# Evening out GpSimd's work over the four steps of an attention group

## The chip, the core and the metric

The kernel runs on one core of a Trainium2 chip. The metric is the device time of one execution in microseconds (us). A core has five engines that work through queues of their own, each in the order in which its instructions were issued: TensorE (PE in the profile; its weight loads are PEld), VectorE (DVE), ScalarE (ACT), GpSimd (POOL) and SyncE (SP, which here only starts transfers). They wait for each other through semaphores. An instruction that waits holds up everything behind it on its engine. Transfers (DMAs) are started from the queues of SP and POOL and then run by themselves.

## What is computed

Eight sequences of 512 tokens with 256 features go through four blocks, each added to its input: attention A, a feed-forward, attention B and the same feed-forward again. All of it is in float32. The change is in attention A only:

```python
# attention A, per token: 16 heads of 64 channels
Q = (x @ Wq + bq).reshape(b, s, H, C) * inv_sqrt_c
K = (x @ Wk + bk).reshape(b, s, H, C)
V = (x @ Wv + bv).reshape(b, s, H, C)
scores = jnp.einsum('bshq,bshk->bshqk', Q, K)
mask = jnp.triu(jnp.ones((C, C), dtype=bool), 1)
scores = jnp.where(mask, jnp.asarray(-jnp.inf, scores.dtype), scores)
w = jax.nn.softmax(scores, axis=-1)
attn = jnp.einsum('bshqk,bshk->bshq', w, V)
...
x = x + _L0_attn_a_ref(_layernorm(x), ...)
x = x + _L0_ffn_ref(_layernorm(x), ...)
x = x + _L0_attn_b_ref(_layernorm(x), ...)
x = x + _L0_ffn_ref(_layernorm(x), ...)
```

This attention is unusual: it works between the 64 channels of one head of one token. Each token and head has its own 64x64 triangle of scores, an outer product of a row of Q and a row of K. There is nothing to multiply as a matrix, so the scores, the exponentials, the products with V and the row sums are element by element work for DVE, GpSimd and ACT.

## The kernel before

Tokens lie on the 128 partitions, so a batch (one sequence) has four tiles of 128 tokens, `i`. The 16 heads are taken in four groups of four heads, `g`, so 256 columns a group. A pair (g, i) is called a group in this text; there are 16 in a batch and 128 in all. The triangle under the diagonal of each head is cut into squares: one of 32x32, two of 16x16, four of 8x8 and so on. A group is worked in four units `u`, one for each step of the schedule (line 553):

- unit 0: the squares of 32 of two heads, in a tile `w` (three buffers, shared with unit 2)
- unit 1: the squares of 16 of all four heads, in a tile `w16` (one buffer)
- unit 2: the squares of 32 of the other two heads, in a tile `w`
- unit 3: the squares of 8, 4, 2 and 1, in a tile `ws` (one buffer)

A tile holds the scores (later their exponentials) and beside them their products with V. Every unit goes through stages, and `step(n)` (line 638) issues one stage of several units, so that units follow each other as in a pipeline. "Step 0" to "step 3" below means a step by the unit whose scores it issues. A step has three parts, with a `yield` after each; between parts the schedule slips in instructions of the other blocks. The stages of a unit are:

- `scores` (line 765): the products of q and k. Units 0 and 2 run on GpSimd, which reads a copy of q and k in SBUF, in two pieces; units 1 and 3 run on DVE, which reads q from PSUM. The group's diagonal (`acc`, L771) goes with unit 0, on DVE.
- `exps` (line 789), one step later: exponentials on ACT.
- `weigh` (line 800), two steps later: products with V on DVE (L808; L805 for the diagonal).
- `halve` (line 810), in the same step: for units 0, 1 and 2 a DMA started by GpSimd adds one half of the tile onto the other (L814, 1 MB).
- `fold` (line 816): for units 0 and 2, GpSimd adds the remaining halves once more (L819). It waits for that DMA.
- `gather` (line 838): DVE sums along the rows (L845). Unit 1's gather waits for unit 1's DMA, those of units 0 and 2 for the folds.
- `add_rows` (line 848): GpSimd adds the sums to the group's numerators and denominators in `acc` (L852). `small_squares` (line 828) is the same for the squares of 2 and 1 on GpSimd.
- `invert` and `divide` (lines 854 and 858): a reciprocal on DVE (L856), once per group, and a product on GpSimd (L860).

The order of PE, DVE, ACT and GpSimd is the order in which this code is called (`manual_schedule`, line 1341); the order on SP is left to the scheduler. For one group, from the calls of `step`, the order in the kernel before is:

| step | DVE | GpSimd |
|---|---|---|
| 0 | weigh 2, diagonal, reciprocal | scores 0 (first piece), start DMA of 2, scores 0 (second piece), divide, fold 0 |
| 1 | weigh 3, gather 1, scores 1 (two pieces), gather 0 | add of the 16s, small squares and their adds, fold 2 |
| 2 | weigh 0, gather 2, gather 3 | scores 2 (first piece), start DMA of 0, scores 2 (second piece), add of unit 0's 32s |
| 3 | weigh 1, scores 3 | start DMA of 1, adds of unit 2's 32s, of the 8s and of the 4s |

The numbers are units; units 2 and 3 in steps 0 and 1 belong to the group before, as do all folds, gathers and adds of sums.

The main loop (lines 1347 to 1354) takes attention A one batch ahead of the other blocks. During the first batch attention A runs alone. From then on, the feed-forward, attention B and second feed-forward of one batch are slipped in between the parts of the next batch's steps (`after_a`, 309.5 units of estimated work for each 64 steps). The last batch's other blocks run alone at the end.

At the beginning there is work that happens once. `fit_qkv` (line 339) subtracts a row from the weights of a head group (on DVE for the first, on GpSimd for the three others) and stores them. `later_weights` (line 411) is a generator, `prep` in the main loop, that prepares other weights: three rounds on a bias row (L421 to L428), products on w3 (L451), on wbqk and wbvp (L456) on GpSimd, and at its end `bound_scores` (line 359), which loads the q, k and v weights again, squares them on ACT (L373 and L374) and sums them on PE (L382), to see whether the scores are bounded. `measure` (line 726) takes the mean and variance of a batch's tokens. Blocks of 8 KB per partition for such data come from a pool of seven (`hp`).

Of the kernel before, what the change touches and what calls it, by code (L numbers as in the profile page):

```python
# [9 lines left out]
F32 = mybir.dt.float32  # L10
# [3 lines left out]
ALU = mybir.AluOpType  # L14
AX = mybir.AxisListType

P = 128
# [9 lines left out]
GW = GH * C  # L27
NG = HID // GW
# [256 lines left out]
def fast_path(ctx: ExitStack, tc: tile.TileContext, k, t, flag):  # L285

    nc = tc.nc
# [8 lines left out]
    ap_ = ctx.enter_context(tc.tile_pool(name="ap", bufs=2))  # L296
# [270 lines left out]
    def pieces(w, n, off, nsq, cols):  # L567

        def of_rows(v):
            return v[:, cols].rearrange("p (x t) -> p x t", t=2 * n)[:, :, n:]

        def of_cols(v):
            return v[:, cols].rearrange("p (x t) -> p x t", t=2 * n)[:, :, :n]

        if n < 16:
            e, ev = (  # L580
                w[:, a * SMALL + off : a * SMALL + off + nsq * n * n].rearrange("p (x i j) -> p x i j", i=n, j=n)
                for a in range(2)
            )
            yield e, ev, lambda v: of_rows(v).unsqueeze(3), lambda v: of_cols(v).unsqueeze(2)
            return
        both = w.rearrange("p (b a x i j) -> p a b x i j", a=2, x=nsq, i=n, j=JB)
        if n == 32:
            for x in range(nsq):
                yield (
                    both[:, 0, :, x],  # L590
                    both[:, 1, :, x],
                    lambda v, x=x: of_rows(v)[:, x].unsqueeze(1).unsqueeze(3),
                    lambda v, x=x: of_cols(v)[:, x].rearrange("p (b j) -> p b j", j=JB).unsqueeze(2),
                )
        else:
            for k in range(n // JB):
                yield (
                    both[:, 0, k],
                    both[:, 1, k],
                    lambda v: of_rows(v).unsqueeze(3),  # L600
                    lambda v, k=k: of_cols(v)[:, :, k * JB : (k + 1) * JB].unsqueeze(2),
                )

    class AttentionA:
# [33 lines left out]
        def step(self, n):  # L638

            weighed = self.at(n - 2)  # L640
            if weighed[0] is not None:
                self.weigh(*weighed)
            unit = self.at(n)
            on_pool = unit[3] in (0, 2)
            if on_pool:
                half = self.scores(*unit)
                next(half)
            if weighed[0] is not None:
                self.halve(*weighed)
            if on_pool:  # L650
                next(half, None)
            b, i, g, u = self.at(n + 40)
            if u == 0 and g == 0 and i == 0 and b > 0:
                self.x[b] = load_x(b)
            b, i, g, u = self.at(n + 10)
            if u == 0 and g == 0 and i == 0:
                self.measure(b)
            b, i, g, u = self.at(n + 8)
            if u == 0 and g == 0:
                self.live["xn"] = normed(self.x[b][:, i, :], *self.rn[b, i], "a")  # L660
            b, i, g, u = self.at(n - 5)
            if u == NU - 1:
                self.invert(b, i, g)
            b, i, g, u = self.at(n - 4)
            if u == 1:
                self.gather(b, i, g, u)
            b, i, g, u = self.at(n + 7)
            if u == 0 and g == 0:
                nc.scalar.copy(self.live[b, i], self.live.pop("ps_ln"))
            if self.at(n - 1)[0] is not None:  # L670
                self.exps(*self.at(n - 1))
            yield
            if unit[0] is not None and not on_pool:
                for _ in self.scores(*unit):
                    pass
            for args in self.sums:
                self.add_rows(*args)
            self.sums = []
            b, i, g, u = self.at(n - 5)
            if u == NU - 1:  # L680
                self.divide(b, i, g)
            b, i, g, u = self.at(n - 2)
            if u == NU - 1:
                self.small_squares(b, i, g)

            b, i, g, u = self.at(n - 4)
            if u == 0:
                self.fold(b, i, g, u)
            b, i, g, u = self.at(n - 3)
            if u == 2:  # L690
                self.fold(b, i, g, u)
            b, i, g, u = self.at(n - 9)
            if u == NU - 1:
                self.new_x(b, i, g)
            b, i, g, u = self.at(n + 2)
            if u == 0:
                self.keep_qk(b, i, g)
            b, i, g, u = self.at(n - 7)
            if u == NU - 1:
                self.turn_group(b, i, g)  # L700
            b, i, g, u = self.at(n - 8)
            if u == NU - 1:
                self.project_out(b, i, g)
            b, i, g, u = self.at(n + 3)
            if u == 0:
                self.project(b, i, g)
            yield
            b, i, g, u = self.at(n - 4)
            if u == 2:
                self.gather(b, i, g, u)  # L710
            b, i, g, u = self.at(n - 5)
            if u == 0:
                self.gather(b, i, g, u)
            b, i, g, u = self.at(n - 3)
            if u == NU - 1:
                self.gather(b, i, g, u)
            b, i, g, u = self.at(n - 7)
            if u == NU - 1:
                nc.scalar.copy(self.live["att"], self.live.pop("pta"))
            b, i, g, u = self.at(n + 8)  # L720
            if u == 0 and g == 0:
                self.live[b, i] = lnp.tile([P, DC, P], F32, tag="xnt_a", name=f"xnta_{b}_{i}", bufs=NT)
                self.live["ps_ln"] = turned_over(self.live.pop("xn"), half_bank().rearrange("p (c s) -> p c s", c=DC))
            yield
# [40 lines left out]
        def scores(self, b, i, g, n_u):  # L765

            qv, kt = self.live[b, i, g][:2]
            if n_u == 0:
                acc = ap_.tile([P, 2, GW], F32, tag="acc", name=f"acc_{b}_{i}_{g}", bufs=3)
                self.live[b, i, g].append(acc)  # L770
                nc.vector.tensor_tensor(acc[:, 0, :], qv[:, 0], kt[:, 0], ALU.mult)  # L771

            if n_u in (0, 2):
                w = wt.tile([P, 4096], F32, tag="w", name=f"w_{b}_{i}_{g}_{n_u}", bufs=3)
            elif n_u == 1:
                w = wt.tile([P, 4096], F32, tag="w16", name=f"w16_{b}_{i}_{g}")
            else:
                w = wt.tile([P, 2 * SMALL], F32, tag="ws", name=f"ws_{b}_{i}_{g}")
            self.live[b, i, g, n_u] = w
            eng, q = (nc.gpsimd, kt[:, 1]) if n_u in (0, 2) else (nc.vector, qv[:, 0])  # L780
            for n, off, nsq, cols in squares(units[n_u]):
                for e, ev, rows, columns in pieces(w, n, off, nsq, cols):
                    shape = list(e.shape)
                    eng.tensor_tensor(  # L784
                        e, rows(q).to_broadcast(shape), columns(kt[:, 0]).to_broadcast(shape), ALU.mult
                    )
                    yield
# [50 lines left out]
        def gather(self, b, i, g, n_u):  # L838


            w = self.live.pop((b, i, g, n_u))
            for n, off, nsq, cols in squares(units[n_u]):
                if n > 2:
                    red = ap_.tile([P, 2, nsq * n], F32, tag=f"red{nsq * n}", name=f"red_{b}_{i}_{g}_{n_u}_{n}", bufs=2 + (n < 32))
                    nc.vector.tensor_reduce(red, self.columns_of(w, n, off, nsq), AX.X, ALU.add)  # L845
                    self.sums.append((b, i, g, n, cols, red))

        def add_rows(self, b, i, g, n, cols, part):

# [491 lines left out]
    with tc.manual_schedule(engines={ET.PE, ET.DVE, ET.Activation, ET.Pool}):  # L1341
        a = AttentionA()
        prep = later_weights()
        fit_qkv(0)
        weights = None
        done, spent = after_a(), 0
        for n in range(-10, a.steps):
            for part, _ in enumerate(a.step(n)):
                if n >= 2:
                    next(prep, None)  # L1350
                while 3 * spent * each < total * (3 * (n - each - 11) + part + 1):
                    spent += next(done)
            if 0 <= n < NG - 1:
                fit_qkv(n + 1)
        for _ in done:
            pass
    judge()
# [86 lines left out]
```

## Time and profile before

| | us |
|---|---|
| median of 3 runs (lowest, highest) | 4008.09 (4007.45, 4010.71) |
| the profiled execution | 4009.55 |
| its span, first to last instruction | 4007.6 |

Some groups of instructions of that execution (a span on GpSimd overlaps with the next by up to 0.3 us, so the distance from start to start is shorter than its mean):

| line, engine, what | count | busy us | mean ns |
|---|---|---|---|
| L784 POOL, scores of units 0 and 2 | 512 | 1076.2 | 2102 |
| L784 DVE, scores of unit 1 | 256 | 301.3 | 1219 |
| L808 DVE, weigh units 0, 1, 2 | 768 | 899.8 | 1213 |
| L819 POOL, folds | 256 | 643.1 | 2512 |
| L814 POOL, start of the adding DMA | 384 | 337.1 | 878 |
| L845 DVE, gathers of units 0 and 2 | 256 | 309.7 | 1210 |
| L845 DVE, gather of unit 1 | 128 | 292.0 | 2281 |
| L852 POOL, adds of 128x256 sums (16s, 8s, 4s) | 384 | 291.6 | 759 |
| L852 POOL, adds of 128x128 sums (32s) | 256 | 179.4 | 701 |
| L856 DVE, reciprocal | 128 | 223.2 | 1744 |

The profile shows for each engine when it was busy, and for each instruction what ended the idle time before it. A row of the timeline has the start and the length in us, the engine, the line of the kernel, the operation, what is written and read, and in brackets the idle time before it with what ended it. Tile names are cut: `w` stands for the tiles of units 0, 1 and 2, `ws` for unit 3. "red" is the sum tile of a gather. Shapes tell the units apart: a gather of 128x1024 from `w` is unit 0 or 2, of 128x2048 from `w` is unit 1.

### The profile page before, as it was taken

What the parts mean: (1) busy time and instruction counts of PE and PEld (TensorE: products, weight loads), DVE (VectorE), ACT (ScalarE), POOL (GpSimd) and SP (SyncE); (2) the same over time, 40 slices, a digit from 0 to 9 for tenths busy, and PEclk for the clock granted to TensorE, in tenths of its full rate; (3) what the DMA queues carried; (4) which work ended last, traced back from release to release, by engine and by line L of the source; (5) the groups of instructions that cost most, each with busy time, mean ns of one, the idle gap of its engine ahead of it and who ended that gap; (6) DMA issues with size and microseconds to landing.
All of it is one profiled execution on the core that took longest, in us unless ns stands there. A gap on an engine that the chain in (4) does not pass through costs nothing.

```text
span 4007.6 us, 37678 instructions
## 1 busy us (share of the span) xinstructions
PE 2958.0 (74%) x12328; PEld 2012.2 (50%) x12328; DVE 3376.7 (84%) x3777; ACT 2337.2 (58%) x3145; POOL 3098.1 (77%) x3051
## 2 busy tenths in 40 slices
PE   1543478777876888768787788768787778768988
PEld 0311145355653656346553566346653556436847
DVE  4899988998889888998989988998889988897115
ACT  2433465666755766666755767567656667555342
POOL 6688888887888887887888888888888878886211
PEclk7555689888987989889897889879898899879999
DMA  8566777668776777668776688668877687767304
GB/s 240 114 141 145 146 182 182 147 161 199 199 162 126 195 188 196 150 147 210 174 192 139 168 198 214 147 131 198 195 181 151 154 199 205 155 133 210 126 29 167
DMA packets 118653, 671.07 MB, mean 167 GB/s; under 512 B 12704, under 2 KB 31915, under 8 KB 43824
## 3 DMA queue, kind: packets, MB, share of 16 engines
q0 software_dynamic: 78336, 570.46, 62.9%
q1 hardware_dynamic: 40112, 98.11, 6.8%
q8 instruction: 100, 1.64, 0.2%
q14 instruction: 105, 0.86, 0.1%
HBM read 255.90 MB, written 9.96 MB: 66 GB/s over the span
## 4 chain that ended last, share of the span: by engine, by line
DVE 38%; PE 16%; POOL 14%; DMA 12%; issue 8%; ACT 8%; POOLq 0%; DVEq 0%; ACTq 0%
DVE red L845 15%; DMA w<-w 12%; DVE w L808 10%; PE ph L1120 5%; ACT w L798 3%; POOL w L819 3%; DVE ws L808 3%; POOL w L784 3%; PE pqkb L1167 3%; DVE ws L784 3%; POOL acc L852 3%; DVE w L784 2%; POOL w L814 2%; DVE acc L856 2%; POOL h L1036 2%
## 5 line engine op out<-in xcount | busy, mean ns | idle before, releaser
L798 ACT ACTIVATE w<-w 128x2048 f32<-128x2048 f32 x384 | 734.2, 1913 | 653.8 <-POOL w L784 440.8
L1120 PE MATMUL ph<-h,hidden 128*128 128x512 f32 x4096 | 1047.9, 412 | 77.4 <-POOL h L1036 45.5
L784 POOL TENSOR_TENSOR w<-k 128x1024 f32<-128x1024 f32 x512 | 1076.2, 2102 | 9.6 <-ACT k L762 9.0
L1120 PEld LDWEIGHTS ph<-h,hidden 128*128 128x128 f32 x4096 | 795.3, 196 | 282.1 <-POOL h L1036 55.9
L808 DVE TENSOR_TENSOR w<-w,qv 128x1024 f32<-128x1024 f32 x768 | 899.8, 1213 | 22.4 <-ACT w L798 22.3
L845 DVE TENSOR_REDUCE red<-w 128x128 f32<-128x1024 f32 (+1 forms) x384 | 601.8, 1567 | 171.6 <-DMA w<-w 94.6
L819 POOL TENSOR_TENSOR w<-w 128x1024 f32<-128x1024 f32 x256 | 643.1, 2512 | 72.5 <-DMA w<-w 71.9
L814 POOL DMA_DIRECT2D w<-w x384 | 337.1, 878 | 339.7 <-issue 134.8
L852 POOL TENSOR_TENSOR acc<-acc,red 128x256 f32<-128x256 f32 (+1 forms) x640 | 471.0, 736 | 152.3 <-DVE red L845 124.5
L845 DVE TENSOR_REDUCE red<-ws 128x256 f32<-128x2048 f32 (+1 forms) x256 | 435.5, 1743 | 0.0
L746 PE MATMUL qv<-wqv,xnta 128*128 128x512 f32 x512 | 299.3, 715 | 89.9 <-DVE ws L808 82.4
L808 DVE TENSOR_TENSOR ws<-ws,qv 128x1024 f32<-128x1024 f32 (+3 forms) x512 | 294.7, 638 | 49.4 <-ACT ws L798 49.4
L1052 PE MATMUL pw<-xnt,gate 128*128 128x512 f32 (+2 forms) x1152 | 298.8, 419 | 24.9 <-ACT silu L1028 18.0
L784 DVE TENSOR_TENSOR w<-qv,k 128x1024 f32<-128x1024 f32 x256 | 301.3, 1219 | 3.6
L784 DVE TENSOR_TENSOR ws<-qv,k 128x1024 f32<-128x1024 f32 (+3 forms) x512 | 299.8, 648 | 0.0
L868 PE MATMUL bank<-ident,acc 128*128 128x128 f32 x256 | 64.3, 341 | 287.5 <-ACT k L761 287.1
L798 ACT ACTIVATE ws<-ws 128x1920 f32<-128x1920 f32 x128 | 231.5, 1809 | 75.3 <-DVE ws L784 74.7
L1052 PEld LDWEIGHTS pw<-xnt,gate 128*128 128x128 f32 x1152 | 227.6, 213 | 82.1 <-ACT silu L1028 22.3
L1229 ACT ACTIVATE eb<-psb 128x256 f32<-128x256 f32 (+3 forms) x512 | 182.2, 443 | 146.6 <-PE psb L1226 146.3
L1146 PE MATMUL pof<-w,h 128*128 128x256 f32 x1024 | 247.9, 396 | 19.4 <-ACT h L1085 19.4
L1085 ACT ACTIVATE h<-ph,s_sb 128x512 fp32r<-128x512 f32 (+1 forms) x256 | 171.1, 688 | 145.9 <-PE ph L1120 144.6
L856 DVE RECIPROCAL acc<-acc 128x256 f32<-128x256 f32 x128 | 223.2, 1744 | 12.3 <-POOL acc L852 12.3
(143 smaller groups left out, 4723.5 us busy)
## 6 DMA issues: line engine op xcount, KB each, us to landing
w<-w POOLq DMA_DIRECT2D x384, 1024.0 KB, 7.7
hidden<-in_h POOLq DMA_DIRECT2D x128, 1024.0 KB, 7.9
gate<-in_w12p POOLq DMA_DIRECT2D x32, 1024.0 KB, 9.0
w<-w_d SPq DMA_DIRECT2D x16, 1024.0 KB, 12.0
wqv<-wqv_d SPq DMA_DIRECT2D x31, 512.0 KB
wo<-in_wo SPq DMA_DIRECT2D x32, 256.0 KB, 7.4
wbqk<-wbqk_d SPq DMA_DIRECT2D x8, 1024.0 KB
w<-in_h SPq DMA_DIRECT2D x8, 1024.0 KB, 7.0
```

Of the source, the lines that this page charges most:

```text
L746: nc.tensor.matmul(qv.rearrange("p j f -> p (j f)"), xnt[:, c, :], wqv[:, c, :], start=(c == 0), stop=(c == DC - 1),)
L784: eng.tensor_tensor(e, rows(q).to_broadcast(shape), columns(kt[:, 0]).to_broadcast(shape), ALU.mult)
L798: nc.scalar.activation(e, e, AF.Exp, scale=C**-0.5)
L808: nc.vector.tensor_tensor(ev, e, columns(qv[:, 1]).to_broadcast(list(e.shape)), ALU.mult)
L814: nc.gpsimd.dma_start(w[:, :2048], w[:, 2048:], accum_op=ALU.add)
L819: nc.gpsimd.tensor_tensor(w[:, :1024], w[:, :1024], w[:, 1024:2048], ALU.add)
L845: nc.vector.tensor_reduce(red, self.columns_of(w, n, off, nsq), AX.X, ALU.add)
L852: nc.gpsimd.tensor_tensor(rows, rows, part.rearrange("p a (x i) -> p a x i", i=n), ALU.add)
L856: nc.vector.reciprocal(acc[:, 0, :], acc[:, 0, :])
L1052: nc.tensor.matmul(pj[:, toks], w[:, m % 4, j, c, :], xs[:, p, c, toks], start=(p == 0 and c == 0), stop=(p == 1 and c == DC - 1),)
L1120: nc.tensor.matmul(pss[j], w[:, j, c, :], h_in(p, c), start=(p == 0 and c == 0), stop=(p == 1 and c == MC - 1),)
L1146: nc.tensor.matmul(po, h(0, c)[:, i * P : (i + 1) * P], w3[:, c, :], start=(c == 0), stop=False)
```

## The change

It has four edits in attention A and one in the main loop. (1) The first of the two score pieces of unit 1 is computed by GpSimd instead of DVE. (2) The sums of units 0 and 2 are written into one tile and added to `acc` together, once, after unit 2's gather. (3) The fold of unit 0 is issued at the end of step 3 instead of in the middle of the following step 0, and its gather at the end of step 0 instead of step 1. (4) The first batch's `measure` is called before the first `fit_qkv`. (5) `prep` takes one step for each step of the kernel (after its third part, from step number 3) instead of one after each part from step number 2, and the last three calls of `fit_qkv` come after step numbers 4, 14 and 24 instead of 0, 1 and 2.

With this, the table of a group reads (moved or new in capitals): step 0, GpSimd without the fold, DVE with GATHER 0 at its end; step 1, GpSimd begins with SCORES 1 (first piece), then the add of the 16s, small squares and fold 2 as before, DVE has one piece of scores 1 and no gather 0; step 2, GpSimd without an add; step 3, GpSimd has one add for all 32s, those of the 8s and 4s, and FOLD 0 at its end.

```diff
--- before.py
+++ after.py
@@ -654,7 +654,8 @@
                 self.x[b] = load_x(b)
             b, i, g, u = self.at(n + 10)
             if u == 0 and g == 0 and i == 0:
-                self.measure(b)
+                if b > 0:
+                    self.measure(b)
             b, i, g, u = self.at(n + 8)
             if u == 0 and g == 0:
                 self.live["xn"] = normed(self.x[b][:, i, :], *self.rn[b, i], "a")
@@ -683,9 +684,6 @@
             if u == NU - 1:
                 self.small_squares(b, i, g)
 
-            b, i, g, u = self.at(n - 4)
-            if u == 0:
-                self.fold(b, i, g, u)
             b, i, g, u = self.at(n - 3)
             if u == 2:
                 self.fold(b, i, g, u)
@@ -706,14 +704,13 @@
                 self.project(b, i, g)
             yield
             b, i, g, u = self.at(n - 4)
-            if u == 2:
-                self.gather(b, i, g, u)
-            b, i, g, u = self.at(n - 5)
-            if u == 0:
+            if u in (0, 2):
                 self.gather(b, i, g, u)
             b, i, g, u = self.at(n - 3)
             if u == NU - 1:
                 self.gather(b, i, g, u)
+            if u == 0:
+                self.fold(b, i, g, u)
             b, i, g, u = self.at(n - 7)
             if u == NU - 1:
                 nc.scalar.copy(self.live["att"], self.live.pop("pta"))
@@ -777,9 +774,11 @@
             else:
                 w = wt.tile([P, 2 * SMALL], F32, tag="ws", name=f"ws_{b}_{i}_{g}")
             self.live[b, i, g, n_u] = w
-            eng, q = (nc.gpsimd, kt[:, 1]) if n_u in (0, 2) else (nc.vector, qv[:, 0])
             for n, off, nsq, cols in squares(units[n_u]):
-                for e, ev, rows, columns in pieces(w, n, off, nsq, cols):
+                for p, (e, ev, rows, columns) in enumerate(pieces(w, n, off, nsq, cols)):
+
+                    on_pool = n == 32 or n == 16 and p == 0
+                    eng, q = (nc.gpsimd, kt[:, 1]) if on_pool else (nc.vector, qv[:, 0])
                     shape = list(e.shape)
                     eng.tensor_tensor(
                         e, rows(q).to_broadcast(shape), columns(kt[:, 0]).to_broadcast(shape), ALU.mult
@@ -841,9 +840,15 @@
             w = self.live.pop((b, i, g, n_u))
             for n, off, nsq, cols in squares(units[n_u]):
                 if n > 2:
-                    red = ap_.tile([P, 2, nsq * n], F32, tag=f"red{nsq * n}", name=f"red_{b}_{i}_{g}_{n_u}_{n}", bufs=2 + (n < 32))
-                    nc.vector.tensor_reduce(red, self.columns_of(w, n, off, nsq), AX.X, ALU.add)
-                    self.sums.append((b, i, g, n, cols, red))
+                    if n_u != 2:
+                        self.live["red", n] = ap_.tile(
+                            [P, 2, GW // 2], F32, tag=f"red{n // 32}", name=f"red{n}_{b}_{i}_{g}", bufs=1 if n == 32 else 3
+                        )
+                    red = self.live["red", n]
+                    part = red[:, :, cols.start // 2 : cols.stop // 2]
+                    nc.vector.tensor_reduce(part, self.columns_of(w, n, off, nsq), AX.X, ALU.add)
+                    if n_u != 0:
+                        self.sums.append((b, i, g, n, slice(0, GW), red))
 
         def add_rows(self, b, i, g, n, cols, part):
 
@@ -1341,17 +1346,18 @@
     with tc.manual_schedule(engines={ET.PE, ET.DVE, ET.Activation, ET.Pool}):
         a = AttentionA()
         prep = later_weights()
+        a.measure(0)
         fit_qkv(0)
         weights = None
         done, spent = after_a(), 0
         for n in range(-10, a.steps):
             for part, _ in enumerate(a.step(n)):
-                if n >= 2:
+                if n >= 3 and part == 2:
                     next(prep, None)
                 while 3 * spent * each < total * (3 * (n - each - 11) + part + 1):
                     spent += next(done)
-            if 0 <= n < NG - 1:
-                fit_qkv(n + 1)
+            if n in (4, 14, 24):
+                fit_qkv(n // 10 + 1)
         for _ in done:
             pass
     judge()
```

## The prediction

> **What bounds the kernel now.** I read the page's busy shares and 40 slices first, then busy time by windows, then the timelines of VectorE (DVE) and GpSimd (POOL) through one group, and last the waits.
>
> ```profile
> PE 2958.0 (74%) x12328; PEld 2012.2 (50%) x12328; DVE 3376.7 (84%) x3777; ACT 2337.2 (58%) x3145; POOL 3098.1 (77%) x3051
> ...
> DVE  4899988998889888998989988998889988897115
> POOL 6688888887888887887888888888888878886211
> ```
>
> DVE is busiest, GpSimd close behind; both fall away only in the last four slices, where the last batch's feed-forward and attention B run alone (TensorE's part, untouched by the change).
>
> ```profile
> 300.00:400.00 100.00, 37.65 (x64) 17.93 (x64) 99.73 (x108) 39.00 (x38) 85.25 (x78) 0.50 0.71 147
> ...
> 1393.90:1424.20 30.30, 25.62 (x98) 20.28 (x99) 23.92 (x26) 21.55 (x23) 22.14 (x20) 0.86 0.82 207
> ```
>
> (Columns: window, its length, busy time of PE, PEld, DVE, ACT, POOL; granted clock, DMA share, GB/s.) Attention A alone keeps DVE 99.7% busy. A group under a feed-forward takes 30.3 us with no engine full. The group's one reciprocal (L856) marks the period: of 127 intervals, 27 are short (mean 23.7 us), 21 middling (25.7, mostly under attention B), 78 long (30.4, feed-forward), and the first is 55.2. Here are DVE and GpSimd in a short group, from step 1 to step 3:
>
> ```profile
> 1250.14 2.29 DVE L845 TENSOR_REDUCE red<-w 128x256 f32<-128x2048 f32 x1 [0.60 <-DMA w<-w]
> 1252.46 2.36 DVE L784 TENSOR_TENSOR w<-qv,k 128x1024 f32<-128x1024 f32 x2
> 1254.73 1.21 DVE L845 TENSOR_REDUCE red<-w 128x128 f32<-128x1024 f32 x1
> 1255.86 0.41 DVE L805 TENSOR_TENSOR acc<-acc,qv 128x256 f32<-128x256 f32 x1
> 1256.19 2.34 DVE L808 TENSOR_TENSOR w<-w,qv 128x1024 f32<-128x1024 f32 x2
> 1258.45 1.21 DVE L845 TENSOR_REDUCE red<-w 128x128 f32<-128x1024 f32 x1
> 1259.58 3.40 DVE L845 TENSOR_REDUCE red<-ws 128x256 f32<-128x2048 f32 x2
> 1262.90 2.34 DVE L808 TENSOR_TENSOR w<-w,qv 128x1024 f32<-128x1024 f32 x2
> ```
> ```profile
> 1252.57 0.73 POOL L852 TENSOR_TENSOR acc<-acc,red 128x256 f32<-128x256 f32 x1 [0.53 <-DVE red L845]
> 1253.26 0.61 POOL L835 TENSOR_TENSOR ws<-ws 128x256 f32<-128x256 f32 x1
> 1253.95 1.66 POOL L852 TENSOR_TENSOR acc<-acc,ws 128x256 f32<-128x256 f32 x2
> 1255.57 2.37 POOL L819 TENSOR_TENSOR w<-w 128x1024 f32<-128x1024 f32 x1
> 1257.90 1.95 POOL L784 TENSOR_TENSOR w<-k 128x1024 f32<-128x1024 f32 x1
> ```
>
> Read them together. At 1252.43 DVE ends the reduce of the squares of 16 ("gather 16"). GpSimd, waiting for it, runs adds, small squares and the second fold until 1257.94. DVE has its own work until 1258.45, when it needs that fold for the reduce at 1258.45 ("gather 2"). The handshake closes with 0.5 us to spare; that margin is what the change touches.
>
> **What the Trainium skill says.** "GPSIMD Engine Reference", section 3.1, has a tensor_tensor of 2048 fp32 at 4497 ns on GpSimd and 2293 ns on VectorE, 1.96 times; here 1024 elements (L784) take 2102 and 1219 ns, 1.72 times: agreed roughly. "Perfetto Trace Analysis", GPSIMD Engine Instruction, advises start-to-start spacing over reported spans; the trace agrees (L784's mean is 2102 ns, the spacing 1.90 to 1.97), so I use spacings. "SBUF — State Buffer", Who interferes with whom, says a DVE tensor_tensor with both inputs in SBUF contends with GpSimd's reads; DVE's half keeps q in PSUM, and the 2.36 us pair above is undisturbed, so I add nothing for it.
>
> **The change, part by part** (spacings from these timelines).
>
> 1. Half of unit 1's scores to GpSimd. DVE loses 1.14 us a group (half of 2.27), GpSimd gains 1.95. The w16 tile has one buffer, so GpSimd's half must wait for gather 16 to have read the previous group's. In the compiled order it stands before the add of the 16s, the small squares and the fold of unit 2, so all of these queue behind that wait.
> 2. One add of 128x256 (0.70) replaces two of 128x128 (0.41 and about 0.7): GpSimd minus 0.4. The single buffer of the shared 32-square sums is free a fold before it is rewritten: nothing.
> 3. Fold of unit 0 (2.35) moves from step 0 to the end of step 3; its DVE reduce ("gather 0", 1.12) from step 1 to step 0. The fold now follows its DMA's issue by about 8 us instead of 13.5 (POOL timeline: issue at 1211.89; adds end at 1220.5; old fold at 1225.68). That DMA lands in 7.1 us (median, 200 to 500 us) and mostly 7.7 to 8.1 in the long groups I looked at. About even; a late landing stalls scores of unit 0 and the next DMA issue behind it.
>
> Sums for a short group: DVE 23.72 - 1.14 = 22.58; GpSimd about 21.1 + 1.95 - 0.4 = 22.6. By busy time alone this is a gain of up to 1.1 us. But follow the handshake. After gather 16, GpSimd needs 0.14 (wait) + 1.95 (its half) + 5.37 (1252.57 to 1257.94, as now) = 7.45 us until the fold ends. DVE's work between gather 16 and gather 2 shrinks from 5.98 to 1.14 + 0.33 + 2.26 = 3.73, since half the scores and gather 0 left that stretch. DVE stalls 3.7 us. Nothing on DVE can overtake, and GpSimd's half cannot start sooner. The closed chain is 7.45 + 18.85 (gather 2 round to the end of the next gather 16: 17.73 now, plus gather 0's 1.12) = 26.3 against 23.72: plus 2.6 us.
>
> Short groups: 27 x 2.6 = 70 us. Middling: ACT or DMA waits on DVE hide some, I take 1.8, 21 x 1.8 = 38 us.
>
> Long groups. DVE now waits for DMA and folds here:
>
> ```profile
> POOL acc L852 <- DVE red L845: 124.5, 57, 23.4
> ...
> DVE red L845 <- DMA w<-w: 94.6, 39, 7.2
> ...
> DVE red L845 <- POOL w L819: 76.9, 30, 5.6
> ```
>
> Three kinds occur between 1300 and 1600 us. Where feed-forward work fills the stretch from gather 16 to gather 2 (13.9 us in one group, 10.6 in another), the longer GpSimd chain is covered, and GpSimd, freed of a fold in step 0, may arrive earlier: 0, or minus 1 to 2. Where that stretch is tight (7.1 us, three groups), plus 0.4 and gather 0's 1.1. Where unit 2's DMA lands late (12.7 to 16.7 us), the fold of unit 0 before its issue delays it by about 2. I bound the mean by minus 1.2 (all of the first kind) and plus 2.5 (all of the third), and take plus 1.0: 78 x 1.0 = 78 us.
>
> 4. The beginning. Now the loads and squares for the bound of the scores come so early that ACT stands in front of them:
>
> ```profile
> 107.15 1.06 ACT L374 ACTIVATE sk<-sk 128x1024 f32<-128x1024 f32 x1 [21.88 <-DMA sk<-in_wqkv]
> ```
>
> DVE then waits 24.7 us for ACT, and the first interval is 55.2 instead of 23.7: 31 us to win. One generator step per kernel step instead of three puts squares at step 19, loads a step ahead. The first moments go ahead of the q/v subtraction: some 3 us more. Against it: the three GpSimd fits (3.6 each) and w3/wbqk products (10) now lie in groups whose GpSimd chain is tight; and on SP's queue the load of w3 stands behind the next wk load, which waits for TensorE's projection, so GpSimd's first w3 product can wait a whole load (7 to 12 us for such loads on the page). I bound the gain by 0 and 35 and take 20.
>
> Sum: 70 + 38 + 78 - 20 = 166 us. The profiled run took 4009.55 us (span 4007.6), the median 4008.09: 4175 either way.
>
> **Rivals.**
> A, not slower: the lighter step 0 decides. If GpSimd is what is late at step 1 in nearly all long groups, moving 2.35 us of fold out and 1.95 in, with DVE's stretch 2.3 shorter, gains 1.2 net: 70 + 38 - 94 - 20 = -6, 4002 us. It decides from a gain of 1.1 us in the mean long group. For it: GpSimd waited for gather 16 in only 57 of 128 groups. Against: GpSimd merely in time already counts among the other 71, as in short groups, where the chain closes. A larger gain needs the short groups' chain not to close too.
> B, slower still: two folds each wait for their DMA in turn. Fold 0, scores, issue, DMA, fold 2, scores, issue, DMA is a ring of L0 + L2 + 8.6 us; in short groups 7.1 + 7.1 + 8.6 = 22.8, harmless, but with 7.9 and 15 it is 31.5 before any feed-forward work on GpSimd (1.3 each, L1036). It decides from L0 + L2 of about 22. Long groups then lose 2.5: 70 + 38 + 195 - 20 = +283, 4291 us. For it: GpSimd already waits 71.9 us for fold DMAs. Against: waiting spreads the DMAs, so that each lands sooner.
> That half the scores do not reach GpSimd is excluded by the compiled order.
>
> **How the numbers follow.** My case 0.71, B 0.18, A 0.11. The predicted time is my case's, 4175. Its long groups from 0 to 2, middling from 1 to 2.5 and beginning from 0 to 35 span 4080 to 4290; with half of B's spread the range is 4080 to 4300, leaving A and B's upper part out. 0.2% is about what a measurement of this kernel can tell from no change; A's 0.11 splits into 0.08 faster (it could also gain in short groups) and 0.03 same.
>
> **What would show it.** Right: reciprocals 26.3 us apart between 200 and 500 us, DVE at about 86% there, about 3.7 us of idle before DVE's reduce of unit 2 put down to GpSimd's fold, GpSimd waiting before its half of the 16 scores, ACT's 21.9 us wait gone. Wrong: short intervals at or below 23.7, or long ones shortened by over a microsecond. B shows as folds of unit 0 waiting on DMA in most long groups.

## The result, and the profile after

The kernel after takes 4197.38 us (median; 4195.32 to 4198.02), the kernel before 4008.87 beside it (4007.45 to 4010.71). The ratio is 1.0469, with a 95% interval of 1.0451 to 1.0487: 188 us slower. First the busy shares and slices of the page:

```profile
PE 2990.4 (71%) x12328; PEld 2029.9 (48%) x12328; DVE 3251.6 (77%) x3649; ACT 2341.4 (56%) x3145; POOL 3316.3 (79%) x3051
...
DVE  6788878888788878888878878888878888887105
...
POOL 7888888888888888888888888888888888887111
```

The load was evened out as intended: DVE has 125 us less to do, GpSimd 218 us more, and the two are about equal. Yet neither is full anywhere. Busy time by windows, in attention A alone, where DVE was 99.7% busy before:

```profile
300.00:400.00 100.00, 37.41 (x64) 17.79 (x64) 87.81 (x98) 34.57 (x35) 87.46 (x71) 0.53 0.62 127
```

Two engines at 87% with nothing else in that stage near its limit: they wait for each other. The timeline of DVE from gather 16 to gather 2 of one group:

```profile
309.78 2.28 DVE L849 TENSOR_REDUCE red<-w 128x256 f32<-128x2048 f32 x1
312.10 1.22 DVE L783 TENSOR_TENSOR w<-qv,k 128x1024 f32<-128x1024 f32 x1
313.24 0.41 DVE L804 TENSOR_TENSOR acc<-acc,qv 128x256 f32<-128x256 f32 x1
313.56 2.35 DVE L807 TENSOR_TENSOR w<-w,qv 128x1024 f32<-128x1024 f32 x2
319.42 1.22 DVE L849 TENSOR_REDUCE red<-w 128x128 f32<-128x1024 f32 x1 [3.51 <-POOL w L818]
```

And GpSimd's over the same stretch:

```profile
312.14 1.95 POOL L783 TENSOR_TENSOR w<-k 128x1024 f32<-128x1024 f32 x1 [0.67 <-DVE red L849]
314.05 0.73 POOL L857 TENSOR_TENSOR acc<-acc,red 128x256 f32<-128x256 f32 x1
314.74 0.61 POOL L834 TENSOR_TENSOR ws<-ws 128x256 f32<-128x256 f32 x1
315.43 1.66 POOL L857 TENSOR_TENSOR acc<-acc,ws 128x256 f32<-128x256 f32 x2
317.05 2.34 POOL L818 TENSOR_TENSOR w<-w 128x1024 f32<-128x1024 f32 x1
```

GpSimd's piece of the 16s starts 0.08 us after gather 16 ends at 312.06, because it must overwrite the tile that this gather read. The adds, the small squares and the fold stand behind it, and DVE sits idle for 3.51 us before gather 2. In the view of the waits (total, times, longest):

```profile
ACT w L797 <- POOL w L783: 844.2, 238, 11.5
DVE red L849 <- POOL w L818: 358.5, 142, 8.2
...
POOL w L783 <- DVE red L849: 174.1, 107, 4.6
...
POOL w L818 <- DMA w<-w: 43.0, 18, 4.7
```

DVE's wait for folds was 76.9 us before. GpSimd's wait for gather 16 was about 122 us before, ahead of the add of the 16s; it now stands ahead of the piece of scores (174.1). The folds' wait for their DMAs fell from 71.9.

The time by groups, from the intervals between reciprocals (classes are those of the kernel before; a sum is the change of all intervals of the class):

| | before, mean | after, mean | change in sum |
|---|---|---|---|
| to the first reciprocal | 86.3 | 73.1 | -13 |
| first interval | 55.2 | 27.5 | -28 |
| 27 short | 23.7 | 26.9 (26.2 from the seventh group on) | +87 |
| 21 middling | 25.7 | 27.3 | +34 |
| 78 long | 30.4 | 31.7 | +103 |
| behind the last reciprocal | 319.2 | 323.7 | +5 |

### The profile page after: what moved, and what is told of

The parts are those of the page before. It is cut to its first block, busy times and chain, and to the rows that moved or that the text cites. A ratio compares the mean times of both kernels' runs of the same rounds, so it can differ in the third digit from the quotient of the medians.

```text
span 4196.2 us, 37644 instructions
## 1 busy us (share of the span) xinstructions
PE 2990.4 (71%) x12328; PEld 2029.9 (48%) x12328; DVE 3251.6 (77%) x3649; ACT 2341.4 (56%) x3145; POOL 3316.3 (79%) x3051
## 4 chain that ended last, share of the span: by engine, by line
DVE 35%; POOL 31%; PE 14%; DMA 8%; issue 7%; ACT 5%; SPq 0%; POOLq 0%; ACTq 0%; DVEq 0%
DVE red L849 16%; POOL w L783 9%; DVE w L807 8%; DMA w<-w 7%; POOL w L818 7%; POOL acc L857 7%; PE ph L1125 4%; DVE ws L807 4%; DVE ws L783 2%; DVE acc L861 2%; ACT w L797 2%; POOL h L1041 2%; PE pqkb L1172 2%; POOL w L813 2%; PE pyb L1239 1%
## 5 line engine op out<-in xcount | busy, mean ns | idle before, releaser
L783 POOL TENSOR_TENSOR w<-k 128x1024 f32<-128x1024 f32 x640 | 1328.8, 2076 | 188.7 <-DVE red L849 174.1
L1125 PE MATMUL ph<-h,hidden 128*128 128x512 f32 x4096 | 1061.8, 416 | 110.9 <-POOL h L1041 72.1
L1125 PEld LDWEIGHTS ph<-h,hidden 128*128 128x128 f32 x4096 | 804.9, 199 | 316.7 <-POOL h L1041 82.3
L818 POOL TENSOR_TENSOR w<-w 128x1024 f32<-128x1024 f32 x256 | 605.4, 2365 | 43.4 <-DMA w<-w 43.0
L857 POOL TENSOR_TENSOR acc<-acc,red 128x256 f32<-128x256 f32 x512 | 410.8, 802 | 27.8 <-DVE red L849 7.9
L783 DVE TENSOR_TENSOR ws<-qv,k 128x1024 f32<-128x1024 f32 (+3 forms) x512 | 299.9, 650 | 0.0
L743 PEld LDWEIGHTS qv<-wqv,xnta 128*128 128x128 f32 x512 | 107.7, 224 | 307.4 <-issue 211.1
L738 PE MATMUL bank<-wk,xnta 128*128 128x256 f32 x512 | 156.7, 433 | 131.1 <-ACT x L892 114.0
```

What stands on the lines that cost most here:

```text
L743: nc.tensor.matmul(qv.rearrange("p j f -> p (j f)"), xnt[:, c, :], wqv[:, c, :], start=(c == 0), stop=(c == DC - 1),)
L783: eng.tensor_tensor(e, rows(q).to_broadcast(shape), columns(kt[:, 0]).to_broadcast(shape), ALU.mult)
L818: nc.gpsimd.tensor_tensor(w[:, :1024], w[:, :1024], w[:, 1024:2048], ALU.add)
L857: nc.gpsimd.tensor_tensor(rows, rows, part.rearrange("p a (x i) -> p a x i", i=n), ALU.add)
L1125: nc.tensor.matmul(pss[j], w[:, j, c, :], h_in(p, c), start=(p == 0 and c == 0), stop=(p == 1 and c == MC - 1),)
```

## The experiments

Two theories: the **closed chain** (called ring in some expectations) of the prediction, in which DVE and GpSimd wait for each other once a group, and **load**: GpSimd's added work costs its time wherever it stands. "Short", "middling" and "long" are the classes above. Before took 4010.6 us beside the first eight runs, 4011.6 and 4013.8 beside the later ones.

**The three parts, each alone on the kernel before.** `begin_only` has edits 4 and 5, `half_only` edit 1, `folds_only` edits 2 and 3. Cut to their core (left out are the moved calls of `fit_qkv` and `measure(0)` in begin_only and the merged sums in folds_only):

```diff
 # begin_only
-                self.measure(b)
+                if b > 0:
+                    self.measure(b)
...
-                if n >= 2:
+                if n >= 3 and part == 2:
                     next(prep, None)
 # half_only
-            eng, q = (nc.gpsimd, kt[:, 1]) if n_u in (0, 2) else (nc.vector, qv[:, 0])
...
+                    on_pool = n == 32 or n == 16 and p == 0
+                    eng, q = (nc.gpsimd, kt[:, 1]) if on_pool else (nc.vector, qv[:, 0])
 # folds_only
-            b, i, g, u = self.at(n - 4)
-            if u == 0:
-                self.fold(b, i, g, u)
...
-            if u == 2:
-                self.gather(b, i, g, u)
-            b, i, g, u = self.at(n - 5)
-            if u == 0:
+            if u in (0, 2):
                 self.gather(b, i, g, u)
...
+            if u == 0:
+                self.fold(b, i, g, u)
```

> The kernel before with only the new beginning (measure first, one preparation step per kernel step, later fits). Both theories: groups from 300 us on stay 23.7 us apart, the first interval between reciprocals falls from 55.2 to about 27 us, GpSimd's moved preparation gives some 10 to 20 us back in the next six groups: 3980 to 3995 us, about 20 below before.

> The kernel before with only half of the scores of the 16s on GpSimd; fold 0 and gather 0 stay where they were. Ring theory (the closed chain from gather 16 over GpSimd's fold 2 to gather 2 and round DVE to gather 16 sets a short group): GpSimd 7.45 us, the rest of the ring 17.74, so 25.2 us for a short group, and 4090 to 4140 us in all. Load theory (GpSimd simply has too much, its own speed decides, the order does not matter): this edit is the whole added load, so short groups at 26.2 us and about 4200 us.

> The kernel before with only the moved fold 0 and gather 0 and the merged sums of the 32s; all scores of the 16s stay on DVE. Ring theory: GpSimd 5.5 us, the rest of the ring 17.74 + 1.12, so 24.4 us for a short group, against DVE's own 23.7; 4030 to 4070 us in all. Load theory: GpSimd has 0.4 us less than before, so 23.7 us and no more than 4009 us.

| | time | ratio, 95% interval | steady short group | change in sum: short, middling, long |
|---|---|---|---|---|
| begin_only | 3993.76 | 0.9958 (0.9942 to 0.9975) | 23.7 | +25, +1, +4 |
| half_only | 4164.26 | 1.0379 (1.0361 to 1.0396) | 25.2 | +40, +21, +85 |
| folds_only | 4064.63 | 1.0131 (1.0109 to 1.0153) | 24.4 | +20, +9, +24 |

The parts add up: -17 + 154 + 54 = 191, against 188 for all. `begin_only` is a gain: the first reciprocal and the first interval are 44 us earlier in all, and the preparation, now spread over the next groups, takes 25 back. The short groups come out at 25.2 and 24.4 as the chain says. The whole of `half_only` is above what I expected (4090 to 4140), because its long groups lose 1.1 us each.

`half_only` confirms the chain less than it seems. GpSimd's timeline has a second wait in the same group:

```profile
319.01 0.87 POOL L815 DMA_DIRECT2D w<-w  x1 [2.28 <-DVE w L809]
```

GpSimd stands before the DMA of unit 1 until DVE has weighed unit 1. From that DMA to the end of the next fold of unit 2 it has 17.8 us of work in order, and DVE 7.3 from gather 2 to the end of that weighing: 25.2 again, so this run can't tell the two chains apart. `folds_only` can. There GpSimd is idle within the second chain, before the add of the 16s:

```profile
316.74 0.73 POOL L854 TENSOR_TENSOR acc<-acc,red 128x256 f32<-128x256 f32 x1 [0.74 <-DVE red L846]
```

Without this wait the second chain would be 23.6, and the measured 24.4 is the first. In after the second is 25.5, hidden 0.7 behind the first.

**GpSimd's piece behind the fold.** `late_half`: after, with GpSimd taking the other piece, behind fold 2, so that the first chain has no scores in it.

```diff
+            rest = ()
             if unit[0] is not None and not on_pool:
-                for _ in self.scores(*unit):
-                    pass
+                rest = self.scores(*unit)
+                next(rest)
...
                 self.fold(b, i, g, u)
+            for _ in rest:
+                pass
...
-                    on_pool = n == 32 or n == 16 and p == 0
+                    on_pool = n == 32 or n == 16 and p == 1
```

> The changed kernel with the same instructions in another order: DVE's piece of the 16 scores is issued where it was, GpSimd's piece after fold 2 instead of before the add of the 16s. Ring theory: GpSimd's share of the ring falls by 1.95 to 5.5 us, so 24.4 us for a short group and 4040 to 4090 us in all. Load theory: same instructions, same load, so 26.2 us and 4197 us as in the changed kernel.

4305.19 us, ratio 1.0733 (1.0715 to 1.0752): the time was a miss by over 200 us. Yet in the first batch, where attention A runs alone, the steady groups are mostly at 24.3 to 24.5 (three at 24.8 to 25.3), as the chain says (the second chain would give 23.6 here). GpSimd does all that it did in after, so load is out as the reason for 26.2. The short groups of the later batches are mostly at 26.4 to 28.8, though, and what got worst is the long groups, 33.1 us. ACT's timeline in one of them:

```profile
2448.05 1.92 ACT L800 ACTIVATE w<-w 128x2048 f32<-128x2048 f32 x1
2457.05 1.91 ACT L800 ACTIVATE w<-w 128x2048 f32<-128x2048 f32 x1 [7.08 <-POOL w L786]
2458.97 1.28 ACT L1093 ACT_TABLE_LOAD   x1
2460.27 0.69 ACT L1093 ACTIVATE h<-ph,s_sb 128x512 fp32r<-128x512 f32 x1
```

ACT stands for 7 us before unit 1's exponential, which waits for the late piece, and the feed-forward's own activation (L1093), for which TensorE waits, stands behind it. Was that the reason? `late_half_late_exp` moves this exponential to the last part of its step:

```diff
-            if self.at(n - 1)[0] is not None:
+            if self.at(n - 1)[3] not in (None, 1):
                 self.exps(*self.at(n - 1))
...
+            if self.at(n - 1)[3] == 1:
+                self.exps(*self.at(n - 1))
```

> late_half (4305 us, long groups 33.1 us) with ScalarE's exponential of unit 1 moved from the first to the last part of its step, behind the work of later stages that is put between the parts. If long groups were slow there because ScalarE, in order, stood before GpSimd's late piece with TensorE's and VectorE's work behind it: long groups come back to about 31 us, groups of attention A alone stay at 24.4 to 25 (VectorE may now meet the exponential at the start of step 3), 4080 to 4200 us in all. If the late piece itself or GpSimd's load was the reason: long groups stay near 33, 4280 us or more.

4219.27 us, ratio 1.0519 (1.0501 to 1.0536): 86 us come back, 49 of them in the long groups and 27 in the short ones, so ACT's order was part of it. But the time is above the range, and the long groups only went to 32.5, not to 31: ACT still waits 912 us for GpSimd's scores, and TensorE now 314 us for the copy of `att`, which has come to stand behind the moved exponential. How the rest divides stays open.

**Four buffers in turn.** If the piece waits only because w16 has one buffer, another buffer takes the wait away. `four_buffers` puts units 0, 1 and 2 on one set of four in place of three and one; memory and the order on the four scheduled engines are those of after.

```diff
-                w = wt.tile([P, 4096], F32, tag="w", name=f"w_{b}_{i}_{g}_{n_u}", bufs=3)
+                w = wt.tile([P, 4096], F32, tag="w", name=f"w_{b}_{i}_{g}_{n_u}", bufs=4)
             elif n_u == 1:
-                w = wt.tile([P, 4096], F32, tag="w16", name=f"w16_{b}_{i}_{g}")
+                w = wt.tile([P, 4096], F32, tag="w", name=f"w_{b}_{i}_{g}_{n_u}", bufs=4)
...
```

> The kernel after with one thing changed: the one buffer of the scores of the 16s and the three of the scores of the 32s become one set of four, used in turn. Same memory, same instructions in the same order on every engine; GpSimd's piece of the 16s no longer waits for VectorE's reduce of the 16s of the group before, but for a reduce that lies most of a step earlier. Closed-chain theory: the piece's 1.95 us leaves the chain, but the merged add, the small adds and the fold stay in it (0.14 + 5.37 on GpSimd, 18.85 on VectorE = 24.4): groups of attention A alone 24.4 us in place of 26.2, middling ones near 26.2, long ones 31.0 or less, in all 4025 to 4105 us. Rival 'GpSimd's added work costs its time wherever it may start' (load, shared access to memory): groups stay at 26.2, 4180 us or more.

4107.27 us, ratio 1.0238 (1.0221 to 1.0255): 90 of the 188 us are gone with no instruction moved or removed, though the time is 2 us above the range. The long groups are at 30.9. The short ones, however, are at 25.5 and not at 24.4: the second chain, which I had not counted. GpSimd's timeline:

```profile
315.65 2.35 POOL L818 TENSOR_TENSOR w<-w 128x1024 f32<-128x1024 f32 x1
...
325.38 0.87 POOL L813 DMA_DIRECT2D w<-w  x1 [2.68 <-DVE w L807]
```

and DVE's:

```profile
318.04 1.22 DVE L849 TENSOR_REDUCE red<-w 128x128 f32<-128x1024 f32 x1 [2.94 <-POOL w L818]
319.17 3.40 DVE L849 TENSOR_REDUCE red<-ws 128x256 f32<-128x2048 f32 x2
322.49 2.34 DVE L807 TENSOR_TENSOR w<-w,qv 128x1024 f32<-128x1024 f32 x2
```

From gather 2 at 318.04 to the DMA at 325.38 are 7.3 us; from the DMA one period earlier (325.38 - 25.5 = 299.9) to gather 2 are 18.2. Together 25.5: each wait feeds the other. (Any two points of a period add up to it. It is a chain because GpSimd has no idle time from 299.9 to the end of that fold, and DVE none from gather 2 to the end of the weighing.)

Two variants, `four_buffers_g0` (gather 0 back in step 1) and `four_buffers_small` (besides, the sums of the 16s added behind fold 2):

```diff
 # both
-            if u in (0, 2):
+            if u == 2:
+                self.gather(b, i, g, u)
+            b, i, g, u = self.at(n - 5)
+            if u == 0:
                 self.gather(b, i, g, u)
 # four_buffers_small
-            for args in self.sums:
-                self.add_rows(*args)
-            self.sums = []
+            if unit[3] != 1:
+                for args in self.sums:
+                    self.add_rows(*args)
+                self.sums = []
...
+            for args in self.sums:
+                self.add_rows(*args)
+            self.sums = []
```

> Four buffers in turn, and the reduce of unit 0 back in step 1, where it was before the change. Closed-chain theory: 5.51 on GpSimd + 17.73 on VectorE = 23.2 us a group, just above the loads of 22.6 on both engines: groups of attention A alone 23.2, about 3990 to 4040 us in all. If they stay at 24.4 or more, the place of that reduce has nothing to do with it and another wait holds the group.

> As four_buffers_g0, and in step 1 GpSimd adds the sums of the 16s behind its fold of unit 2, so that nothing ahead of that fold waits for VectorE's reduce of the 16s. Closed-chain theory: the chain is open; the groups of attention A alone are then set by the loads of 22.6 us, or by the DMA ahead of the fold: 22.6 to 23.4, 3970 to 4030 us in all. Rival: the fold waits for its DMA instead, with the sums behind it: 24 or more and over 4040 us.

Both missed: 4131.37 us (ratio 1.0299, 1.0281 to 1.0316; short groups 25.5) and 4116.57 (1.0261, 1.0244 to 1.0278; short 24.8). Part of the reason is in the compiled addresses: with gather 0 behind the next group's scores of unit 1, the allocator gave unit 1 the same one of the four buffers every time, so these two had again one buffer for the 16s. The second chain fits the rest: 25.5 in the first, and 0.7 less in the second, where one add of 0.7 has left it.

**Both chains opened.** `open_after`: four_buffers with the sums of the 16s behind fold 2 (as in the diff above), and the DMA of unit 1 behind the adds of step 3, which need only DVE's earlier gathers.

```diff
-            if weighed[0] is not None:
+            if weighed[0] is not None and weighed[3] != 1:
                 self.halve(*weighed)
...
                 self.sums = []
+            if weighed[0] is not None and weighed[3] == 1:
+                self.halve(*weighed)
```

> four_buffers (4107 us, 25.5 us a group of attention A alone) with two moves on GpSimd: the DMA of unit 1, which stood ahead of the three adds of step 3 and waited 2.7 us for VectorE, is issued behind those adds; and in step 1 the sums of the 16s are added behind the fold of unit 2. Theory of a second closed chain (in four_buffers GpSimd from that DMA to the end of the fold, 18.1 us, then VectorE from the reduce of unit 2 to the end of its weighing, 7.4: 25.5): the first move takes the wait out of it, the second 0.7 more, so that nothing closed is longer than the loads of 22.6: groups of attention A alone 22.6 to 23.2, long ones 30.9 or less, 4010 to 4075 us in all. If the groups stay at 24.4 or more, the waits were not what held them.

4011.33 us, ratio 1.0002 (0.9994 to 1.0010). With the same instructions as after, in another order and other buffers, all but about 1 of the 188 us is gone. It is still 0.4% slower than begin_only, which has the new beginning and none of the evened load. The long groups take 30.05 us, less than before's 30.37. Busy time by windows:

```profile
300.00:400.00 100.00, 41.44 (x70) 18.88 (x68) 95.81 (x104) 39.66 (x40) 94.91 (x81) 0.50 0.69 142
```

DVE and GpSimd are at 95% each. The short groups of the first batch are mostly at 23.9, not 22.6 to 23.2 (those of later batches at 23.5 to 26); GpSimd's timeline shows what is late next:

```profile
309.10 0.86 POOL L819 DMA_DIRECT2D w<-w  x1
...
316.14 2.36 POOL L824 TENSOR_TENSOR w<-w 128x1024 f32<-128x1024 f32 x1 [1.11 <-DMA w<-w]
```

Fold 0 waits for its DMA, 7.0 us after the issue, and all of GpSimd behind it: 7.0 + 16.9 from that fold to the next such DMA = 23.9. Edit 3 had cut the lead from this issue to the fold from 13.8 us (before) to 8.7 (after); it costs only now that the other chains are gone. So `open_fold` moves fold 0 one place on, behind the first piece of the next scores and the DMA of unit 2:

```diff
+            b, i, g, u = self.at(n - 4)
+            if u == 0:
+                self.fold(b, i, g, u)
             if on_pool:
                 next(half, None)
...
-            if u == 0:
-                self.fold(b, i, g, u)
```

> open_after (4011 us; groups of attention A alone about 23.9, long ones 30.05) with GpSimd's fold of unit 0 taken one place further: from the end of step 3 into step 0, behind the first piece of the next scores and the DMA of unit 2. In open_after that fold waits 1.1 us for its DMA in every group, and a third closed chain fits what is left: DMA of unit 0 from issue to landing 7.0, then GpSimd from that fold to the next such DMA 16.9, together 23.9. Theory: the move takes 2.5 us out of that chain, no closed chain is longer than the loads of 22.6: groups of attention A alone 22.6 to 23.2, long ones 30.1 or less, 3940 to 3985 us in all, below before and below every version so far. Rival: the fold, now later, makes VectorE's reduce of unit 0 wait instead: groups 23.7 or more, 4000 us or more.

4073.60 us, ratio 1.0153 (1.0139 to 1.0167): the rival. GpSimd's timeline

```profile
321.38 0.87 POOL L820 DMA_DIRECT2D w<-w  x1 [1.62 <-DVE acc L775]
321.99 2.63 POOL L825 TENSOR_TENSOR w<-w 128x1024 f32<-128x1024 f32 x1
```

and DVE's

```profile
324.65 1.22 DVE L856 TENSOR_REDUCE red<-w 128x128 f32<-128x1024 f32 x1 [1.82 <-POOL w L825]
```

show a fourth chain. Fold 0 now stands behind the DMA of unit 2, which waits until DVE has weighed unit 2 (ended about 320.8); DVE then waits for that fold before gather 0. From gather 0 round to the end of that weighing DVE has 20.6 us, the way over GpSimd takes 3.8: 24.4, as measured. That the third chain held open_after at 23.9 thus rests on its timeline alone; no run opened it with a gain.

**The same move on the kernel before.** `begin_dma1` is begin_only with the DMA of unit 1 behind the adds, `open_begin` besides with the sums of the 16s behind both folds. Their diffs are those of open_after without the buffers.

> begin_only (3994 us) with the DMA of unit 1 issued behind the adds of step 3. The groups of attention A alone are bound there by VectorE's own 23.7 us: unchanged. If closed chains hold some of the long groups too (30.4 us, with neither engine full), these get shorter: 3970 to 3992. If not: 3988 to 4000.

> begin_dma1 with the sums of the 16s added behind the folds in step 1 as well, so that neither fold stands behind VectorE's reduce of the 16s. Groups of attention A alone 23.7 unchanged; long ones shorter than in begin_dma1 if the chain over that reduce holds some of them: 3960 to 3990; if not 3985 to 4000.

`begin_dma1` takes 3981.64 us, ratio 0.9928 (0.9914 to 0.9941): faster than both kernels, and than begin_only by about 0.3%. Its short groups are at 23.7 and its long ones at 30.17, against 30.42 in begin_only. That fits a chain over this DMA that held some of the long groups of before too, but does not show it. `open_begin` is outside both of its ranges: 4005.11 us, 0.9983 (0.9975 to 0.9992), long groups at 30.39. The later sums lost what the DMA's move had won; why stays open.

## Why the prediction was right, point by point

**The loads and the chain.** The prediction put the two loads at 22.6 us and the chain at 26.3. Measured: 26.2 a group, DVE at 87.81% of the window (86 was named), 3.51 us idle before gather 2 (3.7), GpSimd waiting before its half of the 16s, and ACT's wait before L374 gone. `late_half`, `four_buffers` and `open_after` show that the chains and not the load were the cost. What the prediction missed is the second chain right behind, 25.5 us. It doesn't alter the forecast for after, but a repair of the first chain alone gains 0.7 us a short group there and no more.

**Short and middling groups.** 70 and 38 us were forecast. The short intervals lost 87, but 25 of it is preparation work, as begin_only shows for the same intervals; 62 are left for the chain. The middling lost 34.

**Long groups** are the term that was mis-sized: plus 1.0 us each was taken, 1.3 measured (103 us in place of 78), inside the bounds of minus 1.2 and plus 2.5. Most of the sum's error of 22 us lies here. The working asked only whether the stretch from gather 16 to gather 2 was tight. The half alone costs 1.1 us a long group. The chain over the DMA of unit 1 was not in the working at all, and ACT's waits for the scores of units 0 to 2 rose from 627 us (440.8 for GpSimd's, 186.3 for DVE's) to 844. That waits and no load make this loss is shown: `open_after` has the whole of the change's work and its long groups are shorter than before's. It can be divided, too. With another buffer for the 16s (`four_buffers`) the long groups are only 40 us above before's in sum in place of 103, and with the two moves of `open_after` they are 24 below. A slower TensorE is no large part of it: in these intervals the granted clock was 0.877 after and 0.889 before, and TensorE's busy time rose by 0.2 us each.

**The beginning.** Minus 20 forecast; begin_only gains 17. It comes about otherwise than in the working: 44 us are won up to the second reciprocal (over the upper bound of 35), and 25 given back where the preparation now lies. The feared wait of the first w3 product for a load did not occur; that product (L451) has no idle time before it in after.

**The range.** Its low end was added up wrongly: long groups at 0, middling at 1 and the beginning at 35 give 70 + 21 - 35 = +56, so 4064 and not 4080. The measured time lies far above both.

**Rival A** fell: in folds_only step 0 is lighter with no half added, and it is 54 us slower; in after the long groups got longer. (Of the 57 waits that the prediction read as waits for gather 16, three stand before other adds; it makes no difference.) **Rival B** didn't occur: folds wait 43 us for DMAs where they waited 72. As a limit it was real though, and appeared in open_after, in the form of one fold.

**Contention.** The prediction added nothing for DVE and GpSimd working at once. Right: in open_after, with both at 95%, the window holds the full loads of both in groups of 23.9 us.

## What to carry to other kernels

When two engines work in order and hand data back and forth, the sum of work on each says only how short a period could be. Follow every closed chain, the instruction's own queue included: what stands ahead of it, what that waits for, and back round; the longest sets the period, and the next longest says what a repair can win. Before work is moved to a less loaded engine, see whether it lands between another engine's output and its next input; here order and buffers were worth 186 us. The evened load gained nothing even with these repaired: open_after is no faster than before, and the fastest version, begin_dma1, does without it.

## What the runs showed of the hardware

DVE and GpSimd ran side by side without slowing each other visibly. In the kernel before, one of DVE's products of L808 took 1.21 us on average both where GpSimd was busy for nearly all of it (360 products) and where it was idle for nearly all of it (166). In open_after, with the two at 95.8 and 94.9 us busy in 100, a pair took 2.34 to 2.35 us (before: 2.34 to 2.35), and GpSimd's first piece of scores 1.95 to 1.98 (before: 1.95 to 1.97). The Trainium skill, "SBUF — State Buffer", Who interferes with whom, expects contention where both of DVE's inputs lie in SBUF; these products read one of theirs from PSUM, so the trace does not speak against it.

The adding transfer of 1 MB within SBUF landed 7.0 us after its issue in open_after. It occupies neither engine meanwhile, yet fold 0, which was next in GpSimd's queue, stood 1.1 us for it.
